# Four graph layers on one core: the statistics' small steps move to GpSimd, the last bias becomes a product with ones, new parts and a new order at both ends

## The chip, the cores and the metric

One of the eight cores of a Trainium2 chip runs the whole program. Its engines are PE (TensorE, products), DVE (VectorE), ACT (ScalarE), POOL (GpSimd) and SP, which here only issues DMAs. The metric is the device time of one execution, in microseconds (us). The kernel before took 1287.67 us (median of three runs, 1285.83 to 1288.37).

## The reference, cut to what matters

128 graphs of 128 nodes with 64 features pass four layers. Each layer normalizes its input, applies ReLU and adds its result to x:

```python
h = maximum(layernorm(x), 0)
x = x + L0(h, adj, ...)      # masked sum over neighbours of relu(x_j A + (x_j - x_k) B + b1), then W2
h = maximum(layernorm(x), 0)
x = x + L1(h, adj, ...)      # three relu(adj @ (h W + b)), then Wout
h = maximum(layernorm(x), 0)
x = x + L2(h, adj, ...)      # y = (adj @ h + h) W + b; y /= |y|; batch norm over ALL graphs; relu
h = maximum(layernorm(x), 0)
x = x + L3(h, adj, ...)      # tanh([h, adj @ h] W1 + b1) W2 + b2
```

Only layer 2 ties the graphs together: its mean and variance (per feature) are over all nodes of all graphs, so nothing after it can start until the last graph's y is there.

## The kernel before, in words

The graphs are taken in 32 groups of four (`G = 4`, `NG = 32`). Three stretches follow each other in time.

**The steady run.** For each group, layer 0 sorts neighbours into one-hot matrices (`sort`, `pick`), projects features (`project`), and then works through 40 half tiles: ACT copies a start value into a bank of PSUM (`fill`), PE adds one-hot products to it (`subtract`), DVE takes the ReLU and adds it to `acc` (`gather`). While a group's half tiles run, layers 1 and 2 of the group before it run in the gaps (`after_layer0`: `layer0_end`, `layer1`, `layer2_norm`). `layer2_norm` ends with `add_sums(ysum, ...)`, which collects the sum of y.

**The drain.** When the last gather has ended, the last group's layers 1 and 2 still have to run. This group (31) is split in two halves of two graphs (`SPLIT = 1`, `first_half`, `second_half`). The variance needs the sum of squares of y minus a shift; the shift is the mean over all but the last `BEHIND` groups (`first_mean`, called when group `NG - 1 - BEHIND` has ended, lines 916 and 967). `squares` (line 938) then takes, for each of the 32 groups in turn, one subtraction on DVE, one Square on ACT (tile `sqv`) and two small products on PE (`add_sums(ysq, ...)`, the groups `blk<-nm,sqv`, four columns wide). `filler` (line 956) puts products without a use between them, and `WARM` more (line 1070) follow the last square; they write to free banks. Then come the constants of the batch norm (`factor`, `summand`, lines 1074 to 1084).

**The last phase.** Per group, `add_normed` (line 1115): POOL multiplies and adds the batch norm's constants (`y<-y,affine_g`, two instructions; group 0 does it on DVE), DVE masks the result into PSUM and adds its ReLU to x (`blk<-y,blk`, `x<-blk,x`) and takes `bn_stats`, which give each half row's mean and sum of squares. The groups are put into parts (`PARTS`, line 63). When the last group of a part has its statistics, lines 1146 to 1152 make variance + eps from them in five small DVE steps plus one for the mean (tile `s`), POOL raises it to the power -0.5 (`rstd<-s,halves`), and DVE makes `less`, the negative mean times that. Then `layer3` (line 1161) runs per group: h is made by four ACT instructions (one per graph) or, where `by_vector(g)` holds, by two DVE instructions that read r and the mean from PSUM (`late_ps`); PE multiplies h with the identity and with adjT (`blk<-ident,h`, `blk<-adjT,h`), ACT copies (`hm`), PE applies W1, ACT takes tanh (`tT`), PE applies W2, DVE adds x (`o`), SP writes it out. The last bias is a product of ones with the bias rows (`biased`), except in groups with `by_vector`, where POOL adds it to x (`x<-x,b3o_all`, line 1173).

**What sets the order.** Every instruction that a generator issues stays in program order on its engine (class `InOrder`, line 93, is why nearly all rows stand under L93). The order between generators is planned: each is a `Stream` with a list of due times, and `run_all` (line 1026) lets the stream with the earliest due time take its next step, as far as its gate is open:

```python
            s = min((s for s in streams if s.gate is None or s.gate()), key=lambda s: s.due())
```

So the lists `NORMED_AT`, `LAYER3_AT`, `SQUARES_PLAN`, `FILLER_PLAN`, `SET_UP_PLAN`, `REST_PLAN` and the entries of `MOVED` and `OWN` (shift, scale or a list of its own for one stage of one group) decide which instruction stands before which on each engine, and nothing else.

Of the kernel before, what the change touches and what calls it, by code (L numbers as in the profile page):

```python
# [9 lines left out]
F32 = mybir.dt.float32  # L10
# [3 lines left out]
AF = mybir.ActivationFunctionType  # L14
ALU = mybir.AluOpType
# [3 lines left out]
P = 128  # L19
F = 64  # L20
G = 4
NP = G // 2
# [18 lines left out]
ORDERS = {0: OTHERS[:FULL] + [k for k in ORDER if k not in OTHERS[:FULL]]}  # L41
NORMED_AT = [6, 110, 533, 764, 800, 1146, 1262, 1575, 1754, 2007, 2324, 2362, 2607, 2739, 2914, 3198, 3445, 3602, 3802, 3991, 4178, 4218, 4630, 4782, 4924, 5115, 5299, 5628, 5841, 5841, 6111, 6391]
LAYER3_AT = [-83, 67, 214, 575, 829, 1011, 1234, 1671, 1717, 1817, 2034, 2268, 2463, 2790, 2929, 3113, 3254, 3424, 3558, 3808, 3842, 4197, 4307, 4590, 4983, 4988, 5425, 5463, 5630, 5934, 6438, 6438]
NORMED_PLAN = [-1449, -256, -191, -49, 328, 438, 883]
LAYER3_PLAN = [1024, 1150, 1834, 1931, 2134, 2139, 2139, 2441, 2441, 2672]
MOVED = {('pick', -1): (0, 0.75), ('pick', -2): (-109, 1.102), ('fill', -1): (18, 0.75), ('fill', -2): (0, 1.021), ('subtract', -1): (-1, 0.752), ('subtract', -2): (21, 0.988), ('gather', -1): (0, 0.75), ('gather', -2): (20, 1.0), ('pick', 0): (-1203, 0.997), ('fill', 0): (-119, 0.877), ('subtract', 0): (-65, 0.947), ('gather', 0): (-52, 0.511), ('sort', 0): (-364, 0.972), ('sort', 1): (-635, 0.697), ('project', 0): (691, 0.585), ('project', 1): (155, 0.997), ('after_layer0', 0): (0, 1.0), ('first_half', -1): (-602, 0.992), ('second_half', -1): (-112, 1.0)}
OWN = {('after_layer0', -2): [-734, -65, 691, 691, 691, 691, 691, 972, 1066, 1154, 1255, 1280, 1280, 1440, 1566, 1644, 1757, 1757, 1940, 1940, 2090, 2450, 2450, 2450, 2450, 2685, 2837, 2881, 3086, 3128, 3145, 3290, 3290, 3290, 3438, 3438, 3592, 3592, 3627, 3646, 3684, 3976, 4078, 4109, 4421, 4485, 4512, 4899], ('first_half', -1): [-1189, -966, -886, -871, -753, -659, -570, -311, -230, -110, -107, -26, -26, 24, 49, 159, 231, 233, 351, 355, 454, 465, 465, 520, 582, 606, 717, 717, 879, 909, 909, 998, 1084, 1149, 1238, 1238, 1283, 1313, 1390, 1404, 1404, 1660, 1664, 1695, 1824, 1984, 2001, 3035], ('second_half', -1): [-1130, -987, -834, -703, -655, -586, -484, -231, -231, -231, -109, -52, -17, 45, 104, 176, 245, 361, 361, 365, 470, 482, 482, 541, 607, 632, 750, 783, 934, 968, 968, 1168, 1168, 1222, 1321, 1321, 1368, 1391, 1493, 1493, 1493, 1734, 1786, 1832, 1980, 2117, 2144, 2459], ('sort', 0): [-361, 30, 30, 595, 607, 607, 738, 738, 860, 860, 860, 1135, 1135, 1235, 1331, 1331, 2024, 2074, 2074, 2134, 2159, 2159], ('project', 0): [-1241, -907, -868, -728, -442, 1053, 1192, 3091, 3728, 3875, 4077, 4162, 4162, 4162, 4182, 4512, 4589, 4619, 4619, 4651, 4662, 4902, 4978, 4996, 5074, 5127, 5127, 5664, 5780], ('pick', -1): [-1123, -774, -706, -706, -634, -425, -425, -96, -84, 631, 881, 881, 896, 1076, 1084, 1544, 1671, 1732, 2021, 2039, 2044, 2391, 2680, 2783, 2937, 3043]}
SET_UP_PLAN = [93, 1417, 1908, 1908, 2104, 2104, 3420, 4777]
PERIOD = 3386
# [6 lines left out]
AFTER_PLAN = [-115, -109, 110, 147, 311, 768, 891, 1024, 1031, 1342, 1462, 1486, 1666, 1825, 1907, 2009, 2138, 2138, 2250, 2401, 2571, 2571, 2663, 2805, 2902, 2973, 3117, 3221, 3537, 3748, 3892, 3907, 4155, 4155, 4155, 4239, 4331, 4381, 4557, 4586, 4665, 4760, 4834, 4915, 5251, 5412, 5494, 5494]  # L56
WARM = 15
BEHIND = 2
SPLIT = 1
REST_PLAN = [-107, -107, 444, 444, 444, 444, 447, 597, 1070, 1895, 2111, 2252, 2268, 2268, 2337, 2501, 2510, 2510, 2510, 2520, 2520, 2945, 2945, 2945, 2991, 3251, 3251, 3251, 3254, 3454, 3584, 3584, 3584, 3584, 3959, 4006]  # L60
SQUARES_PLAN = [2562, 2562, 2682, 2742, 2802, 2858, 2912, 2978, 2978, 3094, 3150, 3273, 3295, 3295, 3411, 3411, 3507, 3882, 3896, 3975, 4046, 4342, 4343, 4343, 4348, 4423, 4452, 4528, 4602, 4678, 4753, 4845, 4891, 4891, 4891, 4891, 4891, 5296, 6393, 6393, 6393, 6393, 6393, 6465, 6756, 6814, 6825, 6942, 7471, 7471, 7572, 7644, 7731, 7826, 7918, 8015, 8114, 8210, 8306, 8306, 8477, 8477, 8635, 9169, 9259, 9350, 9520, 9604, 9604, 9687, 9791, 9826, 9899, 9983, 9996, 10065, 10136, 10136, 10142, 10142, 10142, 10168, 10246, 10246, 11277, 11277, 11277, 11277, 11277, 11277, 11277, 11277, 11277, 11277, 11378, 11378, 11410, 11498, 11538, 11694]
FILLER_PLAN = [3597, 3621, 3621, 3627, 3627, 3786, 3786, 3786, 4060, 4060, 4150, 4150, 4150, 4176, 4545, 4605, 4665, 4665, 4665, 4665]
PARTS = [1, 3, 4, 4, 4, 4, 4, 4, 4]
NBLK = 5
# [44 lines left out]
def network(ctx, tc, io, out, over=None, x1=None):  # L109
# [273 lines left out]
    def bias_all(name, src):  # L383

        n = src.shape[0]
        t = keep.tile([P, n], F32, name=name)
        load_later(t, src.rearrange("(o n) -> o n", o=1).broadcast_to([P, n]))
        return t

    gamma_all = bias_all("gamma_all", io["L2_gnn_gamma"])  # L390
    beta_all = bias_all("beta_all", io["L2_gnn_beta"])
    b3o_all = bias_all("b3o_all", io["L3_gnn_b2"])

# [16 lines left out]
    def over_g(ap):  # L410

        return ap.unsqueeze(1).to_broadcast([P, G, F])
# [5 lines left out]
    def flat(t):  # L418
        return t.rearrange("p a n -> p (a n)")
# [59 lines left out]
    def biased(name, width, pt=None, times=G):  # L479

        pt = bank("ps_pr") if pt is None else pt
        matmul(pt[:, 0 : times * width].rearrange("p (b d) -> p b d", d=width), ones_b, bias(name, times), start=True, stop=False, skip_group_check=True)
        return pt
# [602 lines left out]

    nm_ps, y_ps, late_ps = blks[0][:, 0:P], blks[0][:, P : P + G * F], blks[1][:, 0 : 2 * len(PARTS) * G]
    y_ps = y_ps.rearrange("p (b f) -> p b f", f=F)
# [9 lines left out]
    def by_vector(g):  # L1098
        gs = parts[part_of[g]]
        return len(gs) > 1 and g == gs[-1]  # L1100

# [13 lines left out]
    def add_normed(g):  # L1115
# [28 lines left out]
        s1 = work.tile([P, NG // 4, G], F32, tag="var", name="s1")[:, 0 : len(gs), :]  # L1144
        nc.vector.tensor_tensor(s0, stats[:, :, :, 1], stats[:, :, :, 4], ALU.subtract)
        nc.vector.scalar_tensor_tensor(s0, s0, 0.25, s0, ALU.mult, ALU.mult)
        nc.vector.tensor_tensor(s1, stats[:, :, :, 2], stats[:, :, :, 5], ALU.add)
        nc.vector.scalar_tensor_tensor(s0, s1, 1.0 / F, s0, ALU.mult, ALU.add)
        nc.vector.tensor_scalar(s0, s0, LN_EPS, None, ALU.add)
        nc.vector.tensor_tensor(s1, stats[:, :, :, 1], stats[:, :, :, 4], ALU.add)  # L1150
        if by_vector(g):
            nc.vector.tensor_tensor(late_ps[:, 1, k, :], stats[:, len(gs) - 1, :, 1], stats[:, len(gs) - 1, :, 4], ALU.add)
        yield
        nc.gpsimd.tensor_tensor(r, s0, halves[:, 0 : len(gs), :], ALU.pow)
        yield
        nc.vector.scalar_tensor_tensor(less, s1, -0.5, r, ALU.mult, ALU.mult)
        if by_vector(g):
            nc.vector.tensor_copy(late_ps[:, 0, k, :], r[:, len(gs) - 1, :])
        rooted.add(k)

    def layer3(g):
# [6 lines left out]
        if by_vector(g):  # L1168
            r, less = (late_ps[:, n, part_of[g], :] for n in range(2))
            nc.vector.scalar_tensor_tensor(ys[g], over_f(less), -0.5, xs[g], ALU.mult, ALU.add)  # L1170
            relu_scaled(ys[g], r, h=h)
            yield
            nc.gpsimd.tensor_tensor(xs[g], xs[g], over_g(b3o_all), ALU.add)
        else:
            for b in range(G):
                nc.scalar.activation(h[:, b, :], xs[g][:, b, :], AF.Relu, bias=less3[:, g, b : b + 1], scale=rstd3[:, g, b : b + 1])
                if b == 1:
                    yield
# [19 lines left out]
        tT = work.tile([P, NP, P], F32, tag="tT", name="tT")  # L1198
        nc.scalar.activation(flat(tT), pt[:, 0 : NP * P], AF.Tanh, bias=b3p)
        free_ends.append(pt)  # L1200
        yield ENDS
        po = free_ends.pop(0)
        if not by_vector(g):
            biased("L3_gnn_b2", F, pt=po)
        project_pairs(po, tT, w3o, F, start=by_vector(g))
        headed.add(g)
# [169 lines left out]
```

## Time and profile before

| what | us |
|---|---|
| median of three runs | 1287.67 |
| the profiled execution | 1288.35 |
| its span, first to last instruction | 1286.6 |
| last gather add of group 0, of group 30, of group 31 | 70.51, 1094.27, 1128.87 |
| period of a group in the steady run | 34.07 |
| last product of the squares' sum | 1180.18 |
| first and last POOL instruction of the last phase's powers | 1188.03, 1262.6 |
| last PE product of the last group | 1277.9 |

Busy times over the span: PE 1159.5, DVE 1158.9, ACT 1034.2, POOL 318.4 us. In the last phase, from 1182 to 1287, they are PE 76.7, DVE 78.2, ACT 63.5, POOL 72.7 us. "PEclk" in the profile is the TensorE clock that was granted, 1.00 or 0.50 in every stretch of this trace. A stretch is read by asking which engine's next instruction everyone else waits for; the busy share says where to look, the waits say whether it is so. The second copy of the network in the program (`x1` given) belongs to a branch that these inputs do not take.

### The profile page before, as it was taken

Reading aid. Unit: us, or ns where it says so; the run is one execution under the profiler, and the core shown is the slowest. Engines: PE = TensorE matmul, PEld = TensorE weight load, DVE = VectorE, ACT = ScalarE, POOL = GpSimd, SP = SyncE. Lnnn points to the kernel's source line nnn. Section 1 sums busy time; section 2 is a strip of 40 time slices with the busy share of each in tenths; the row PEclk is TensorE's granted clock in tenths of the full one; section 3 lists DMA queues with packets and bytes.
Section 4 is the critical chain, followed back from the end, with each engine's and each line's share of the span. In section 5 each row is a group of like instructions: output and inputs, shape, how many; then the busy total and the mean of one; then the engine's idle time right before and its main releaser. Section 6 shows DMA issues by size and latency. Waiting matters only on the chain.

```text
span 1286.6 us, 31407 instructions
## 1 busy us (share of the span) xinstructions
PE 1159.5 (90%) x10989; PEld 982.1 (76%) x10990; DVE 1158.9 (90%) x3204; ACT 1034.2 (80%) x2583; POOL 318.4 (25%) x400
## 2 busy tenths in 40 slices
PE   5689999999999999999999999999999999888697
PEld 2568888888877887787878878888878887767576
DVE  6889999999999999999999999999999998845993
ACT  3678888888988888888888888888988888743576
POOL 4241122212121222222211222221211222021992
PEclk9899999999999999999999999999999999995899
DMA  2222222222222222222222222222222212100264
GB/s 80 81 76 70 73 67 73 76 76 77 76 76 69 71 74 66 66 74 71 72 74 71 68 71 72 77 76 76 77 76 67 70 59 61 30 17 1 79 160 128
DMA packets 107012, 92.53 MB, mean 72 GB/s; under 512 B 45135, under 2 KB 90460, under 8 KB 106844
## 3 DMA queue, kind: packets, MB, share of 16 engines
q1 hardware_dynamic: 106380, 90.17, 24.7%
q8 instruction: 89, 1.46, 0.5%
q14 instruction: 79, 0.65, 0.2%
q10 hardware_dynamic: 464, 0.26, 0.1%
HBM read 34.12 MB, written 16.71 MB: 40 GB/s over the span
## 4 chain that ended last, share of the span: by engine, by line
ACT 40%; PE 35%; DVE 16%; issue 4%; POOL 2%; SPq 2%; DMA 1%; DVEq 0%; ACTq 0%; POOLq 0%
ACT blk L93 22%; PE blk L93 14%; PE ps_pr L93 7%; DVE acc L93 4%; ACT extra L93 3%; PE ps_q L93 3%; PE ps_ag L93 3%; ACT dT L93 3%; ACT msg L93 2%; PE ps_ah L93 2%; DVE var L93 2%; ACT psort L93 2%; PE ps_ga L93 2%; PE ps_endps L93 2%; SPq L93 2%
## 5 line engine op out<-in xcount | busy, mean ns | idle before, releaser
L93 DVE SCALAR_TENSOR_TENSOR acc<-blk,acc 128x384 f32<-128x384 f32 x1152 | 590.3, 548 | 28.3 <-PE blk L93 21.0
L93 ACT COPY blk<-psort 128x384 f32<-128x384 f32 x1088 | 497.6, 487 | 14.9 <-DVE acc L93 11.5
L93 PE MATMUL blk<-q,oh 128*128 128x192 bf16 x3072 | 321.9, 248 | 9.2 <-ACT blk L93 4.6
L93 PEld LDWEIGHTS <-oh 128*128 128x128 bf16 x3072 | 262.4, 99 | 43.7 <-issue 30.3
L93 PE MATMUL blk<-near_q,ohn 128*128 128x192 bf16 x1536 | 227.7, 247 | 35.9 <-ACT blk L93 32.3
L93 PEld LDWEIGHTS <-ohn 128*128 128x128 bf16 x1536 | 142.8, 99 | 94.9 <-issue 83.3
L93 POOL TENSOR_TENSOR x<-x,t 128x260 f32<-128x260 f32 (+1 forms) x33 | 23.9, 726 | 426.8 <-DVE t L93 372.7
L93 ACT COPY blk<-psort_r 128x384 f32<-128x384 f32 x192 | 89.1, 490 | 1.9 <-DVE acc L93 0.8
L93 ACT COPY zT<-ps_ga 128x256 f32<-128x256 f32 (+1 forms) x31 | 11.4, 369 | 87.5 <-PE ps_ga L93 87.5
L93 POOL TENSOR_TENSOR y<-y,nrm 128x256 f32<-128x256 f32 x31 | 20.4, 657 | 245.4 <-PE blk L93 214.9
L93 PE MATMUL ps_ag<-adjT,msg 128*128 128x128 f32 x500 | 73.7, 280 | 0.5 <-ACT msg L93 0.5
L93 PE MATMUL ps_pr<-g,dT 128*128 128x128 f32 x496 | 72.9, 279 | 0.3 <-ACT dT L93 0.2
L93 DVE TENSOR_SCALAR ohn<-near_n 128x1536 bf16<-128x1536 bf16 (+1 forms) x132 | 72.0, 546 | 0.0
L93 PEld LDWEIGHTS ps_pr<-g,dT 128*128 128x128 f32 x496 | 65.0, 191 | 4.4 <-ACT dT L93 1.6
L93 PEld LDWEIGHTS ps_ag<-adjT,msg 128*128 128x128 f32 x500 | 63.3, 192 | 0.9 <-ACT msg L93 0.7
L93 ACT ACTIVATE dT<-ps_ag 128x512 f32<-128x512 f32 (+1 forms) x96 | 56.5, 588 | 8.6 <-PE ps_ag L93 8.6
L93 DVE SCALAR_TENSOR_TENSOR h<-x,rstd 128x256 f32<-128x256 f32 (+1 forms) x98 | 51.9, 530 | 9.8 <-PE ps_ga L93 2.0
L93 ACT ACTIVATE sq<-x 128x256 f32<-128x256 f32 (+1 forms) x98 | 40.4, 412 | 25.1 <-DVE x L93 25.0
L93 POOL TENSOR_TENSOR q<-rest,q 128x768 bf16<-128x768 f32 x32 | 52.7, 1648 | 18.2 <-ACT q L93 18.2
L93 PE MATMUL ps_q<-wq,hT 128*128 128x384 f32 x128 | 55.5, 518 | 1.4 <-ACT hT L93 1.4
L93 PE MATMUL ps_p<-wp,hs 128*128 128x384 f32 x128 | 53.8, 503 | 0.1
L93 PE MATMUL ps_sA<-fro,acc 128*128 128x128 f32 x256 | 50.7, 280 | 1.3 <-DVE acc L93 1.3
(267 smaller groups left out, 2605.0 us busy)
## 6 DMA issues: line engine op xcount, KB each, us to landing
near_q<-q SPq DMA_DIRECT2D x288, 63.0 KB
near_n<-n_dram SPq DMA_DIRECT2D x96, 126.0 KB
a<-in_adj_dram SPq DMA_DIRECT2D x32, 256.0 KB
adjT_dram<-adjT SPq DMA_DIRECT2D x32, 256.0 KB
adjT<-adjT_dram SPq DMA_DIRECT2D x32, 256.0 KB
psort_r<-psort SPq DMA_DIRECT2D x32, 228.0 KB
fro_r<-fro SPq DMA_DIRECT2D x32, 152.0 KB
x<-in_x_dram SPq DMA_DIRECT2D x32, 128.0 KB
```

Of the source, the lines that this page charges most:

```text
L93: ins = op(*args, **kw)
```

## The change

Five things are edited.

1. `add_normed`: DVE keeps two of the small steps (the sum of the two halves' squares, now in a tile `s2`, and the sum of the two means); the difference of the means, its square, a scale with eps and the sum with `s2` go to POOL, ahead of the power. All is scaled by F, and tanh's `scale=math.sqrt(F)` undoes it.
2. `by_vector` holds for the odd groups among the last eight (four groups) and no longer for the last group of each of eight parts.
3. The last bias is a product with ones in all 32 groups; the load of `b3o_all` and POOL's eight additions go.
4. `PARTS` has again nine parts, now of 1, 3, 4, 5, 5, 5, 5, 2 and 2 groups.
5. The order: `BEHIND` 2 to 1, `WARM` 15 to 24, all entries of `MOVED` and `OWN` for the last two groups are gone, and new lists stand in `NORMED_AT`, `LAYER3_AT`, `NORMED_PLAN`, `LAYER3_PLAN`, `SET_UP_PLAN`, `REST_PLAN`, `SQUARES_PLAN`, `FILLER_PLAN` and in the entries for groups 0 and 1. The plans of the steady run are not touched.

```diff
...
-WARM = 15
-BEHIND = 2
+WARM = 24
+BEHIND = 1
 SPLIT = 1
...
-PARTS = [1, 3, 4, 4, 4, 4, 4, 4, 4]
+PARTS = [1, 3, 4, 5, 5, 5, 5, 2, 2]
+ENDING = 8
...
-    b3o_all = bias_all("b3o_all", io["L3_gnn_b2"])
...
     def by_vector(g):
-        gs = parts[part_of[g]]
-        return len(gs) > 1 and g == gs[-1]
+        return g >= NG - ENDING and g % 2 == 1
+
+    late_at = {g: n for n, g in enumerate(g for g in range(NG) if by_vector(g))}
...
-        nc.vector.tensor_tensor(s0, stats[:, :, :, 1], stats[:, :, :, 4], ALU.subtract)
-        nc.vector.scalar_tensor_tensor(s0, s0, 0.25, s0, ALU.mult, ALU.mult)
-        nc.vector.tensor_tensor(s1, stats[:, :, :, 2], stats[:, :, :, 5], ALU.add)
-        nc.vector.scalar_tensor_tensor(s0, s1, 1.0 / F, s0, ALU.mult, ALU.add)
-        nc.vector.tensor_scalar(s0, s0, LN_EPS, None, ALU.add)
+        s2 = work.tile([P, NG // 4, G], F32, tag="nrm", name="s2")[:, 0 : len(gs), :]
+        nc.vector.tensor_tensor(s2, stats[:, :, :, 2], stats[:, :, :, 5], ALU.add)
         nc.vector.tensor_tensor(s1, stats[:, :, :, 1], stats[:, :, :, 4], ALU.add)
-        if by_vector(g):
-            nc.vector.tensor_tensor(late_ps[:, 1, k, :], stats[:, len(gs) - 1, :, 1], stats[:, len(gs) - 1, :, 4], ALU.add)
-        yield
+        for q, other in enumerate(gs):
+            if by_vector(other):
+                nc.vector.tensor_tensor(late_ps[:, 1, late_at[other], :], stats[:, q, :, 1], stats[:, q, :, 4], ALU.add)
+        yield
+        nc.gpsimd.tensor_tensor(s0, stats[:, :, :, 1], stats[:, :, :, 4], ALU.subtract)
+        nc.gpsimd.tensor_tensor(s0, s0, s0, ALU.mult)
+        nc.gpsimd.tensor_scalar(s0, s0, 0.25 * F, F * LN_EPS, ALU.mult, ALU.add)
+        nc.gpsimd.tensor_tensor(s0, s0, s2, ALU.add)
         nc.gpsimd.tensor_tensor(r, s0, halves[:, 0 : len(gs), :], ALU.pow)
         yield
         nc.vector.scalar_tensor_tensor(less, s1, -0.5, r, ALU.mult, ALU.mult)
-        if by_vector(g):
-            nc.vector.tensor_copy(late_ps[:, 0, k, :], r[:, len(gs) - 1, :])
+        for q, other in enumerate(gs):
+            if by_vector(other):
+                nc.vector.tensor_copy(late_ps[:, 0, late_at[other], :], r[:, q, :])
         rooted.add(k)
...
-            nc.gpsimd.tensor_tensor(xs[g], xs[g], over_g(b3o_all), ALU.add)
...
-        nc.scalar.activation(flat(tT), pt[:, 0 : NP * P], AF.Tanh, bias=b3p)
+        nc.scalar.activation(flat(tT), pt[:, 0 : NP * P], AF.Tanh, bias=b3p, scale=math.sqrt(F))
...
-        if not by_vector(g):
-            biased("L3_gnn_b2", F, pt=po)
-        project_pairs(po, tT, w3o, F, start=by_vector(g))
+        biased("L3_gnn_b2", F, pt=po)
+        project_pairs(po, tT, w3o, F, start=False)
...
```

In the built order of the changed kernel, engine by engine, the steady run (groups 3 to 29) has the same instructions in the same order. Around the first groups, two more half tiles' products stand on PE ahead of group 1's `ps_num`, and three of the constants' loads stand on SP behind group 1's `n_dram`, `near_n` and `fro_r`. In the drain, both halves of group 31 close layer 0 together after the last gather; the squares come as a block of twelve groups (behind the second product of group 31's layer 1 on PE), then four, two and one, and the last thirteen at the end.

## The prediction, on record before the run

> **What bounds the kernel now.** I read the slices first. PE and DVE stay near full up to slice 37, so the steady run fills nine tenths of the span; the order listing shows it unchanged, and I cost it at nothing: the same instructions in the same order, at 34.07 us a group. What can move is the first 70 us, the drain and the last phase.
>
> ```profile
> PE   5689999999999999999999999999999999888697
> POOL 4241122212121222222211222221211222021992
> PEclk9899999999999999999999999999999999995899
> ```
>
> PEclk falls to 5 where the drain ends, and POOL turns from 2 to 9 right after it. So I asked for busy times by stretch: the last group's gather, the drain to the last y product, the squares, the constants, the last phase to its eighth power, the rest. Columns: length, then PE, PE's weight loads, DVE, ACT, POOL, then the granted clock.
>
> ```profile
> 1094.27:1128.87 34.60, 28.82 (x263) 24.83 (x260) 28.63 (x77) 23.08 (x57) 3.19 (x4) 0.95 0.09 26
> 1128.87:1159.84 30.97, 27.90 (x204) 22.41 (x204) 12.14 (x46) 15.52 (x51) 6.71 (x11) 0.96 0.06 19
> 1159.84:1179.50 19.66, 19.21 (x91) 19.12 (x91) 7.61 (x26) 8.48 (x21) 0.00 (x0) 0.50 0.00 0
> ...
> 1191.12:1256.30 65.18, 50.73 (x629) 43.16 (x630) 59.44 (x254) 45.03 (x115) 60.27 (x66) 0.89 0.45 123
> 1256.30:1286.60 30.30, 22.26 (x294) 19.21 (x293) 10.31 (x41) 17.96 (x46) 4.93 (x4) 0.90 0.47 125
> ```
>
> The third row is PE alone, on the squares at half clock. In the fifth POOL and DVE are both over 90% full and PE is not; in the sixth POOL has almost stopped and PE runs out its backlog. The waits from 1182 on (waiter, what it waited for, total, times, longest) give DVE's part in it:
>
> ```profile
> POOL rstd L93 <- DVE s L93: 6.9, 9, 2.7
> ...
> PE blk L93 <- DVE h L93: 3.1, 2, 1.7
> ...
> PE ps_endps L93 <- DVE h L93: 1.9, 1, 1.9
> ```
>
> **Start: -1 us.** DVE's idle time after 28 us, ahead of its adds, is 3.8 to 4.1 us, most of it one wait for products:
>
> ```profile
> 44.31 0.56 DVE L93 SCALAR_TENSOR_TENSOR acc<-blk,acc 128x384 f32<-128x384 f32 x1 [2.26 <-PE blk L93]
> ```
>
> Two more half tiles now stand on PE ahead of group 1's `ps_num`; two adds (2 x 0.56) fit into the 2.26. Group 1's own chain is the later for it, but it is due a period later. On SP three loads of constants move behind group 1's `n_dram`, `near_n` and `fro_r`, which can only start the sooner. Bounds: all of the idle time gained, -3.8; two half tiles lost again at group 1, +1.
>
> **Drain: +5 us.** The terms, in order.
>
> (a) Last gather. With `BEHIND` 1 the shift is computed after it. Before, it stood inside: PE waited 1.8 us for the sums, DVE 0.7 and 0.6 for the results, and DVE spent 1.4 on its steps, 4.5 us in all. This gather took 34.60, a steady one 34.07, so not all of it cost time; the extra products of the redrawn lists move too. I take -3.5 (bounds -6 and 0).
>
> (b) The squares. Before, a group's four products cost 0.51 in the gaps and 0.853 in the final run:
>
> ```profile
> 1136.81 0.51 PE L93 MATMUL blk<-nm,sqv 128*128 128x4 f32 x4
> ```
> ```profile
> 1161.87 17.17 PE L93 MATMUL blk<-nm,sqv 128*128 128x4 f32 x80
> ```
>
> 80 products in 17.17 us is 0.215 each against 0.13 at full clock. 20 groups were left for the end, now 13. Seven stand earlier, in a block of twelve behind group 31's second layer-1 product. I followed the new order from the gather's end G with durations of before: the last message is ready at G+17.5, the shift at G+19.3, and the block ends at G+26.5 at full clock or G+30.4 at half. The granted clock of before lies at half after clock windows of 3.41 us with 3328 streamed columns or fewer (f32 counted four times), at full after 3620 or more; the block streams 4 columns at a time, so I take most of it at half, G+29. `ps_ag` of layer 1, which is what everything else of group 31 waits for, stands behind it: 29 - 17.5 = 11.5 us late. This is the new wait; queued behind it are ACT's `dT`, the two `gout`, `ga`, `py` and `counted`, and nothing else that could fill PE.
>
> (c) From `ps_ag` to `counted`: 14.4 before (1145.49 to 1159.84) with one half left; now both halves go together, at half clock at first: 17.4 (bounds +1 and +5).
>
> (d) Tail: 13 x 0.853 = 11.1 and 2.0 for the last products, where 20 x 0.853 and 2.3 stood.
>
> The sum: G + 17.5 + 11.5 + 17.4 + 13.1 = G+59.5, against 51.3 before, which is +8.2; less 3.5 of (a) +4.7, taken as +5. The bounds: block at full clock (-4), chain +1 instead of +3 (-2), and the gather's -6 with one more for the tail's first products at full clock, -6.6 in all; the other way +1.4, +2 and +3.5, +11.6. The 24 fills of `WARM` cost nothing as long as they end ahead of the first h, which came 10.4 us behind the last `own` product (1180.2 to 1190.6); 24 at some 0.3 are 7 to 8.5.
>
> The Trainium skill says, in "TensorE: Matmul & The Clock Gate", Part 1, that the half clock comes after an idle window of about 3.4 us. The trace differs: the clock stood at half from 1157.4 to 1184.7 while PE was recorded 98% busy, on products four columns wide. By the page's words the block would run at full clock and the sum would be 3 to 4 us less.
>
> **Last phase: -1 us.** POOL's side first:
>
> ```profile
> L93 POOL TENSOR_TENSOR y<-y,affine_g 128x256 f32<-128x256 f32 x62 | 44.2, 730 | 27.3 <-DVE affine_g L93 25.5
> L93 POOL TENSOR_TENSOR rstd<-s,halves 128x16 f32<-128x16 f32 x7 | 20.4, 2910 | 5.8 <-DVE s L93 5.8
> ```
>
> y stays. Powers of 4, 12 and 16 elements took 1.04, 2.28 and 2.91, so 0.156 an element: 20 make 3.54, 8 make 1.66 (estimates), and the nine parts sum to 23.7 as before. The eight bias additions go, -5.5. New are 9 x 4 = 36 small steps. POOL's small steps of before are at the start:
>
> ```profile
> 4.32 0.19 POOL L93 TENSOR_TENSOR caps<-caps,in_n 128x2 f32<-128x2 f32 x1
> 4.61 0.21 POOL L93 TENSOR_SCALAR in_n<-neg_p 128x1 f32<-128x1 f32 x1
> ```
>
> From start to start 0.29, so 10.4 us; with 20 elements instead of 2 and DVE beside them they may take 0.7 (DVE's own step with 16 elements took up to 0.74 while POOL ran y), 25 us. I take 0.29, from the nearer row. POOL: 44.2 + 23.7 + 10.4 = 78.3, plus 3.3 to 5 of waits where 6.9 stood, from 1182.5 on: the last power ends at 1264.6 to 1266 (1262.6 before).
>
> The Trainium skill's "GPSIMD Engine Reference", section 4.1, speaks against this move: two-input steps belong on VectorE, since GpSimd is about half as fast. DVE's steps here came 0.20 apart when undisturbed; twice that is 14.4 us, 4 more than above.
>
> DVE: per part it loses four steps of some 0.3, it makes h for four groups instead of eight (0.84 each), and has no other new work than two small copies per such group: 78.2 becomes about 62.7. It is no longer near the bound; `blk`, `x` and `stats` follow y without queue. PE's 5.0 us of waits for DVE's h go for about half, since POOL's pace (78.3/32 = 2.45 a group) is now what is late next and PE needs 2.2 to 2.3.
>
> ACT gets four more groups' h at 1.46, 5.8 us, in part hidden: it had 63.5 of 105 us. The eight bias products more on PE (0.11 to 0.28 each) cost 1 to 2 us of its sum. PE's backlog at the end: before, the eighth power ended at 1256.3 with eight groups' work left, 1256.3 + 8 x 2.2 = 1273.9 against 1277.9 measured; now the sixth is estimated at 1244.5 with fourteen left, 1275.3. That is +1.4; with -2.5 of the waits, -1. Bounds -5 (all waits gone, POOL no later) and +6 (small steps at 0.45 with no wait saved).
>
> **Sum.** -1 + 5 - 1 = +3 on the profiled 1288.35 (span 1286.6 and 1.75 around it): 1291.4. The median is 0.7 less than that execution; I leave it in.
>
> **Rivals.**
> 1. *DVE was the bound, and the change frees it* (faster, about 1282). For it: `DVE s` is 5.4% of the last 187 us' chain, 10 us, and each part's six steps take up to 2.3 us there, stretched beside POOL's y. If the chain per part gets 0.6 to 1 us shorter, nine parts and the 2.5 of the h give -8; drain +3, start -1: 1282.4. It decides if the last power ends by 1262. Against it: POOL is 92% full already, and it gets more.
> 2. *No measurable difference* (within 0.2%, 2.6 us, about what a measurement of this kernel tells from no change): the block runs at full clock and term (b) shrinks by 4, the rest as forecast: 1287.5. That the change does not do what it says would look the same: the steps leave DVE, whose wait was covered anyway.
> 3. *POOL's small steps are slow* (slower, about 1299): at 0.5 each beside a busy DVE, 36 cost 18 us instead of 10.4; POOL is full from 1191 on, so the last power ends at 1273 and, with the drain's +5, the end comes 10 us later. It decides from 0.4 a step on. For it: DVE's small steps stretched from 0.17 to 0.74 beside y; against it: POOL's y itself shows 0.71 to 0.77 with DVE busy or idle.
>
> **Chances.** The forecast (+2.6 to +8) 0.34, rival 3 and a drain at its upper bound 0.13, rival 2 0.22, rival 1 0.31. So slower 0.47, same 0.22, faster 0.31. The range reaches to rival 1's middle and to rival 3: 1280 to 1299.
>
> **What would show it.** Start: the 2.26 ahead of the add at 44.31 gone and group 0's last add before 70.5. (a): the last gather 34 us or less from the one before. (b): one block of 48 `sqv` products before group 31's `ps_ag`, at 0.21 each if the half clock holds, 0.13 if not; the last `own` product at G+59.5. Last phase: the small steps at 0.29, the powers of 20 at 3.5, the last power at 1266 plus the drain's shift, and PE's waits for DVE's h at half. I am wrong if the block ends before the last message needs PE, or if PE is not the last engine to run out after the last power.

## The result, and the profile after

The changed kernel took 1300.75 us (median of five runs, 1299.76 to 1301.55) against 1288.37 for the kernel before in the same job: ratio 1.0099, 95% interval 1.0085 to 1.0114. It is slower by about 12.5 us, where +3 was forecast and 1299 was the end of the range. The profiled execution has a span of 1299.8 us, 13.2 more than before.

The same slices of the page, of the kernel after:

```profile
PE   5689999999999999999999999999999999796786
...
POOL 3331112222121211222222221112222122014981
PEclk7799999999999999999999999999999999976898
```

In slice 39, the middle of the last phase, PE and POOL both read 8 where they read 9, and in slice 40 PE has 6 for 7: both have become less busy in a phase that has become longer. The stretches that answer to those of before (last gather; drain to the last y product; the last squares; the last phase from the first h product to the eighth power; the rest), same columns:

```profile
1093.72:1129.11 35.39, 28.60 (x264) 24.75 (x262) 27.78 (x69) 24.16 (x57) 3.19 (x4) 0.95 0.09 26
1129.11:1170.31 41.20, 37.59 (x235) 31.32 (x233) 16.14 (x59) 18.52 (x58) 6.63 (x11) 0.79 0.06 14
1170.31:1183.48 13.17, 12.62 (x58) 12.53 (x58) 5.21 (x19) 5.43 (x14) 0.00 (x0) 0.50 0.00 0
1193.78:1268.51 74.73, 56.70 (x683) 47.70 (x683) 52.27 (x214) 54.76 (x146) 65.51 (x91) 0.86 0.41 112
1268.51:1299.80 31.29, 20.16 (x248) 17.07 (x246) 10.97 (x36) 13.21 (x31) 3.88 (x8) 0.84 0.41 109
```

Read the lengths first. Drain and squares together are 54.4 us (50.6 before), the phase up to the eighth power 74.7 (65.2 before). In that row POOL was busy 60.3 of 65.2 us before and is busy 65.5 of 74.7 now: its work grew by 5.2 us, and its idle time nearly doubled, from 4.9 to 9.2 us. DVE fell from 59.4 to 52.3 us of work, in a longer stretch. POOL's share fell from 92% to 88%, so no engine has become the bound by being full. The waits of the kernel after, from 1182 on, say what fills the gaps:

```profile
ACT h L94 <- DVE less L94: 26.5, 5, 8.2
...
DVE less L94 <- POOL rstd L94: 18.0, 9, 3.2
...
POOL s L94 <- DVE stats L94: 7.4, 6, 2.4
...
PE ps_endps L94 <- ACT hm L94: 4.0, 1, 4.0
...
PE blk L94 <- DVE h L94: 2.6, 1, 2.6
```

The second line did not exist before: at each of the nine powers DVE stands and waits for POOL. The third is POOL waiting for DVE. The two wait for each other in turn, and behind them wait ACT's h (18.4 us for `less` before, 26.5 now) and PE.

A fixed point makes runs comparable: the end of the last `ident,own` product (the squares' sum is there), and from it to the end of the last `o` on DVE. The 13.2 us split into the last gather's end +0.24 (1128.87 to 1129.11), from there to that product +3.8 (51.3 to 55.1), from it to the last `o` +8.7 (98.8 to 107.5), and +0.5 behind that. Each value of this measure comes from one profiled execution. Three kernels with the last phase of before gave 98.8, 98.3 and 97.9, and four with that of after 107.2 to 108.0, so a difference of less than 1 us says nothing. The device times of the kernel before scatter more, from 1285.7 to 1290.5 us over its executions.

### The profile page after: what moved, and what is told of

Same layout as the page of the kernel before. It is cut to its first block, busy times and chain, and to the rows that moved or that the text cites. A ratio compares the mean times of both kernels' runs of the same rounds, so it can differ in the third digit from the quotient of the medians.

```text
span 1299.8 us, 31438 instructions
## 1 busy us (share of the span) xinstructions
PE 1167.3 (90%) x11006; PEld 988.0 (76%) x11007; DVE 1147.5 (88%) x3152; ACT 1038.2 (80%) x2599; POOL 322.3 (25%) x428
## 4 chain that ended last, share of the span: by engine, by line
ACT 38%; PE 32%; DVE 18%; issue 6%; POOL 3%; SPq 2%; DMA 1%; DVEq 0%; ACTq 0%; POOLq 0%
ACT blk L94 20%; PE blk L94 13%; PE ps_pr L94 6%; DVE acc L94 4%; PE ps_q L94 3%; ACT extra L94 3%; PE ps_ag L94 3%; ACT msg L94 2%; PE ps_ah L94 2%; ACT dT L94 2%; DVE var L94 2%; ACT psort L94 2%; PE ps_ga L94 2%; POOL rstd L94 2%; SPq L94 2%
## 5 line engine op out<-in xcount | busy, mean ns | idle before, releaser
L94 PE MATMUL blk<-q,oh 128*128 128x192 bf16 x3072 | 322.2, 249 | 11.2 <-ACT blk L94 4.3
L94 ACT ACTIVATE sq<-x 128x256 f32<-128x256 f32 (+1 forms) x98 | 40.1, 410 | 30.8 <-DVE x L94 27.7
L94 ACT ACTIVATE h<-x,less,rstd 128x64 f32<-128x64 f32 x112 | 40.9, 435 | 28.8 <-DVE less L94 26.5
```

Source lines behind the costliest of these rows:

```text
L94: ins = op(*args, **kw)
```

## The experiments

| kernel | ratio to before, 95% interval | own to last o, us | DVE's wait for rstd, us |
|---|---|---|---|
| before | | 98.8 | 0 |
| after | 1.0099 (1.0085 to 1.0114) | 107.5 | 18.0 |
| new start | 0.9989 (0.9975 to 1.0003) | 98.3 | 0 |
| new drain | 1.0024 (1.0015 to 1.0034) | 97.9 | 0 |
| new last phase | 1.0151 (1.0128 to 1.0175) | 107.2 | 18.0 |
| before, steps on POOL | 1.0047 (1.0028 to 1.0066) | 102.5 | 4.0 |
| before, bias product | 0.9988 (0.9975 to 1.0000) | 96.9 | 0 |
| after, steps on DVE | 1.0078 (1.0057 to 1.0100) | 104.4 | 10.3 |
| after, parts of before | 1.0107 (1.0090 to 1.0125) | 105.8 | 18.1 |
| after, lists of normalisation and parts of before | 1.0058 (1.0043 to 1.0073) | 101.5 | 10.6 |
| after, all four lists and parts of before | 1.0031 (1.0018 to 1.0044) | 100.2 | 7.9 |
| before, one list of after | 1.0077 (1.0060 to 1.0094) | 108.6 | 8.4 |

**1 to 3: which end of the kernel.** Start alone:

```diff
-SET_UP_PLAN = [93, 1417, 1908, ...]
+SET_UP_PLAN = [-291, 1261, 1323, ...]
-REST_PLAN = [-107, -107, 444, ...]
+REST_PLAN = [4, 6, 632, ...]
...
```

and so on for the entries of groups 0 and 1 in `MOVED` and `OWN`.

> The kernel before with the new lists of the start alone (set-up, rest, groups 0 and 1). The profile after ends group 0's gather 0.55 us later and group 1's 0.23 sooner than before. Theory (start costs nothing): within 1 us of before. Rival (a start that is later shifts all that follows): +1 to +3 us.

Group 0 ended at 70.25, group 1 at 102.93 (105.26 before), ratio 0.9989. DVE's wait of 2.26 us at 44.31 became one of 1.01. The gain is 1.4 us by the ratio, with an interval that still holds zero; the rival is out. Drain alone:

```diff
-WARM = 15
-BEHIND = 2
+WARM = 24
+BEHIND = 1
...
```

with `SQUARES_PLAN` and `FILLER_PLAN` of after, and without the entries of the last two groups in `MOVED` and `OWN`.

> The kernel before with the drain redrawn alone (shift over all but the last group, 24 fills, the new lists of squares and fills, no own entries for the last two groups). In the profile after the last own product ends 4.05 us later than before, at 1184.23. Theory (the drain is a loss of its own that adds to the last phase's): last own product 4 us later than before, time +3 to +5 us. Rival (the last phase has slack for it): own product 4 us later, time within 1.5 us of before.

The gather ended at 1126.95, 1.9 us sooner than before, but 1.35 of that were there when group 30 ended (1092.92 for 1094.27), in a stretch whose order is that of before. The last own product came at 1182.06, 1.9 later, as 55.1 us lay between. Time +3 us. The drain is a loss of its own. The last phase alone:

```diff
-PARTS = [1, 3, 4, 4, 4, 4, 4, 4, 4]
+PARTS = [1, 3, 4, 5, 5, 5, 5, 2, 2]
+ENDING = 8
-    b3o_all = bias_all("b3o_all", io["L3_gnn_b2"])
...
```

with the four lists of that phase, the steps, the bias and `by_vector` of after.

> The kernel before with the last phase changed alone: small steps on GpSimd, bias as a product, new parts, DVE's h for other groups, new lists of that phase. In the profile after the stretch from the last own product to the last o is 8.7 us longer. Theory (the last phase carries two thirds of the loss, whatever the drain does): +7.5 to +10 us. Rival (the new last phase was drawn for the new drain and loses only behind it): +2 to +5 us.

From own to the last o it took 107.2 us: the loss is there without the new drain. But the ratio of 1.0151 holds another 8 us from the start, which I had not foreseen: with the load of the bias rows gone, the set-up has a step less, the later ones each take an earlier place in the old plan, and DVE waited 9.48 us for one row of constants (0.57 before):

```profile
51.29 0.21 DVE L94 TENSOR_REDUCE cat<-cat 3x1 f32<-3x64 f32 x1 [9.48 <-DMA cat<-in_L_gnn_bout_dram]
```

Group 0 ended at 78.94. From here on the load stays, unused, wherever the old start is combined with the new bias.

**4: is it lost in `after` too?** The kernel after with the load kept:

```diff
+    b3o_all = bias_all("b3o_all", io["L3_gnn_b2"])
```

> The kernel after with the load of the bias rows kept, unused, as last of the later loads, as in the kernel before. Group 0 and 1 ended at 71.06 and 105.03 after, but at 70.25 and 102.93 with the new lists of the start and the load kept. Theory (the load's removal moves every later step of the set-up to another place in the plan, and that is where the gain of the start went): group 1 ends at about 103, time 1 to 2.5 us less than after. Rival (the start's difference is chance of one execution): within 0.7 us of after.

Group 1 ended at 103.93, ratio 1.0098 (1.0075 to 1.0121): the time did not move, so the theory fell. With the new lists of the start, group 1 ended between 102.75 and 105.03 in fourteen profiled executions, with the load and without, 102.75 to 102.93 in ten of them; the 105.03 of after was the latest.

**5 and 6: the small steps.** On the kernel before:

```diff
-        nc.vector.tensor_tensor(s0, stats[:, :, :, 1], stats[:, :, :, 4], ALU.subtract)
-        nc.vector.scalar_tensor_tensor(s0, s0, 0.25, s0, ALU.mult, ALU.mult)
...
+        nc.gpsimd.tensor_tensor(s0, stats[:, :, :, 1], stats[:, :, :, 4], ALU.subtract)
+        nc.gpsimd.tensor_tensor(s0, s0, s0, ALU.mult)
...
```

> The kernel before with the four small steps per part on GpSimd alone; its parts, its h on DVE, its bias additions and its order are those of before. 36 steps at 0.29 us start to start make POOL's own work 10.4 us longer. Theory (the loss of the last phase comes from the parts and the order, 5 5 5 5 2 2, whose round trips between POOL and DVE no longer overlap): +0 to +3 us, the steps' time taken from POOL's 6.9 us of waits and DVE's freed time. Rival (POOL is full, so its added work is the loss): +6 to +9 us, last power 6 to 9 us later.

Own to the last o went from 98.8 to 102.5, the last power from 82.4 (84.0 in the runs of the start and of the drain alone) to 88.2 us behind own, the time up by 6 us: nearer to the rival, POOL had little room. Its waits did shrink: 6.9 us for DVE's `s` before, 2.2 for `stats` here. The price of a step was that of the prediction, 0.29 to 0.32 from start to start and 2.91 for the power, here in this kernel:

```profile
1225.98 0.24 POOL L93 TENSOR_TENSOR s<-stats 128x16 f32<-128x16 f32 x1
1226.30 0.22 POOL L93 TENSOR_TENSOR s<-s 128x16 f32<-128x16 f32 x1
1226.60 0.20 POOL L93 TENSOR_SCALAR s<-s 128x16 f32<-128x16 f32 x1
1226.89 0.22 POOL L93 TENSOR_TENSOR s<-s,s 128x16 f32<-128x16 f32 x1
1227.19 2.91 POOL L93 TENSOR_TENSOR rstd<-s,halves 128x16 f32<-128x16 f32 x1
```

The other way round, in the kernel after:

```diff
-        nc.gpsimd.tensor_tensor(s0, stats[:, :, :, 1], stats[:, :, :, 4], ALU.subtract)
...
+        nc.vector.tensor_tensor(s0, stats[:, :, :, 1], stats[:, :, :, 4], ALU.subtract)
...
```

> The kernel after with the four small steps per part back on DVE, scaled as before; everything else as after. From the last own product to the last o: 98.8 us before, 102.5 with the steps on GpSimd alone, 107.5 after. Theory S (the steps' place and the new parts are two losses that add): 103 to 104.5, time 3 to 4.5 us less than after. Rival P (the parts of five and two set the pace by their round trips, wherever the steps run): 106 to 109, time within 1.5 us of after. Rival D (DVE needs the relief): more than 109.

104.4: theory S. The steps cost 3.1 us here and 3.7 to 4.6 there (102.5 against the three values from 97.9 to 98.8). The time, though, fell only by a ratio of 1.0099 to 1.0078, about 2.7 us, with overlapping intervals; the row of the last phase is the better witness.

**7 and 8: the bias as a product, and a version that beats both.**

```diff
-            nc.gpsimd.tensor_tensor(xs[g], xs[g], over_g(b3o_all), ALU.add)
-        if not by_vector(g):
-            biased("L3_gnn_b2", F, pt=po)
+        biased("L3_gnn_b2", F, pt=po)
```

> The kernel before with the last bias as a product in all 32 groups and GpSimd's eight additions gone; the load of the bias rows stays, unused, so that the set-up keeps its order. Theory A (POOL's pace sets the last phase, 5.5 us of its work go, 3.9 of it ahead of the last power): last power 2 to 4 us sooner, time -1.5 to -4 us. Theory B (PE's backlog sets the end, so POOL's relief is worth nothing and eight more products cost): 0 to +1.5 us.

Own to the last o 96.9, 1.0 to 1.9 less; the eighth power came 1.3 us sooner and the ninth 0.4. Ratio 0.9988 (0.9975 to 1.0000): the time is at the low end of theory A, but its last power, 2 to 4 us sooner, did not come. POOL's additions went, and its waits for DVE's `s` rose from 6.9 to 9.8 us. With the new start as well:

> As the kernel with the bias as a product and the unused load kept, with the new lists of the start added, which alone gave a ratio of 0.9989. If the two are independent: the sum of both, -3 to -6 us by theory A of the bias, -0.5 to -2 us by theory B.

Ratio 0.9979 (0.9967 to 0.9990), 2.7 us less than before, between the two forecasts; it is the lowest ratio of this study and faster than both kernels. Own to the last o 96.9 again, group 1 at 102.76.

**9: the choice of groups whose h DVE makes**, on that kernel:

```diff
-        gs = parts[part_of[g]]
-        return len(gs) > 1 and g == gs[-1]
+        return g >= NG - ENDING and g % 2 == 1
```

> The kernel with the new lists of the start and the bias as a product (load kept), and now h on DVE for every other of the last eight groups, four instead of eight. 96.9 us from own to the last o without this edit. Theory (DVE is the bound up to the eighth power and loses 4 x 0.84 of work, ACT has room): 95.5 to 97. Rival (ACT's four more groups at 1.46 us each stand in PE's way): 97.5 to 100.

97.5 us, ratio 0.9988 (0.9978 to 0.9998): at the border of the two expectations, and no gain that could be measured.

**10 to 12: the parts.** My first theory of the remaining loss was the two short parts at the end, each with a round trip of its own (POOL, kernel after):

```profile
1259.70 3.55 POOL L94 TENSOR_TENSOR rstd<-s,halves 128x20 f32<-128x20 f32 x1
1263.22 1.53 POOL L94 TENSOR_TENSOR y<-y,affine_g 128x256 f32<-128x256 f32 x2
1265.72 0.21 POOL L94 TENSOR_TENSOR s<-stats 128x8 f32<-128x8 f32 x1 [0.97 <-DVE stats L94]
...
1268.48 1.53 POOL L94 TENSOR_TENSOR y<-y,affine_g 128x256 f32<-128x256 f32 x2
1272.41 0.21 POOL L94 TENSOR_TENSOR s<-stats 128x8 f32<-128x8 f32 x1 [2.40 <-DVE stats L94]
```

One group's y, a wait for DVE, a power, the next group's y, a wait. Merged:

```diff
-PARTS = [1, 3, 4, 5, 5, 5, 5, 2, 2]
+PARTS = [1, 3, 4, 5, 5, 5, 5, 4]
```

> The kernel after with its last two parts of two groups made one part of four (1 3 4 5 5 5 5 4); lists, GpSimd's steps and all else as after. From the power of group 28 to that of group 32 it took 6.3 us before and 12.0 after. Theory R (a part's y may only be issued once the part before the last has its rstd, so the two short parts at the end run one round trip of POOL, DVE, POOL after the other): one round trip less, last power 2 to 4 us sooner, from own to the last o 104 to 106 instead of 107.5, time -1.5 to -3.5 us against after. Rival B (PE's backlog of nine groups sets the end, the last power is early enough): time within 1 us of after.

The last power came 90.2 us behind own instead of 91.0, own to the last o stayed at 107.8, ratio 1.0093 (1.0071 to 1.0116): theory R fell. With the last y brought forward too:

```diff
-NORMED_AT = [..., 6242, 6248, 6518, 6847]
+NORMED_AT = [..., 6000, 6100, 6200, 6300]
```

> As the kernel with the last part of four, and the normalisation of the last four groups given earlier due times, so that POOL makes five and a half groups' y ahead of the sixth five-group power and only half a group's after it. Theory R: a further 1 to 3 us less to the last power, 102 to 105 from own to the last o. Rival Y (the y that are brought forward delay the power of groups 23 to 27, for which PE waits): no gain over the merged part, or up to 2 us more.

108.5 us, ratio 1.0126 (1.0107 to 1.0146): the power of groups 23 to 27 came 1.9 us later, as rival Y had it. The parts of before in the kernel after:

```diff
-PARTS = [1, 3, 4, 5, 5, 5, 5, 2, 2]
+PARTS = [1, 3, 4, 4, 4, 4, 4, 4, 4]
```

> The kernel after with the parts of before (1 3 4 4 4 4 4 4 4); its lists, its steps on GpSimd, its h on DVE for every other of the last eight groups as after. The steps on GpSimd alone gave 102.5 from own to the last o, the bias as a product took 1.9 off (98.8 to 96.9). Theory K (the sizes of the parts are the remaining 7 us): 100 to 103, time 4 to 7 us less than after. Rival O (the new order of the lists is it, since POOL has y only two groups ahead at each power where before had three to four): 105 to 108, time within 2 us of after.

105.8: rival O. Part sizes by themselves are at most 1.7 us, and the times do not show them: the ratio is 1.0107 (1.0090 to 1.0125), no lower than that of after, and the profiled execution, at 1296.71 us, was the fastest of four (the others 1300.33 to 1302.31).

**13 to 17: the order.** In the built order of before, POOL has 4, 8, 12, 16, 20, 24, 28, 32 and 32 groups' y made when it comes to the nine powers: always a whole part ahead, so that DVE has that part's `blk`, `x` and `stats` to do while POOL raises to the power. After, the lead is 3, 7, 10, 15.5, 20, 26, 30, 31, 32 for parts that end with 1, 4, 8, 13, 18, 23, 28, 30 and 32 groups. One number first:

```diff
-NORMED_PLAN = [-1606, -170, -126, -89, 175, 181, 411]
+NORMED_PLAN = [-1606, -170, -126, -89, 175, 181, 800]
```

> The kernel after with one number changed: the due time of the step that issues a part's small GpSimd steps and power, 411 to 800 (before: 883). In the built order POOL then has 4, 8, 12, 18, 21, 28, 30, 32, 32 groups' y made ahead of the nine powers, where after had 3, 7, 10, 15.5, 20, 26, 30, 31, 32 and before 4, 8, 12, ... 32, 32. Theory L (the lost lead of the y is the open 5 us: POOL and DVE wait for each other in turn): DVE's waits for rstd, 18.0 us after, fall below 8, and own to the last o falls from 107.5 to 102.5 to 105.5. Rival H (the choice of groups for DVE's h, or the sizes of the parts): above 106.5.

108.5 us, ratio 1.0104 (1.0087 to 1.0121): theory L failed here. DVE's wait for rstd fell from 18.0 to 9.6 us, but POOL's y now waited 6.9 us for DVE to be done with an older y, and the power of the first five-group part ended 44.5 us behind own instead of 40.0. The same with the parts of before:

> As the kernel with 411 changed to 800, and with the parts of before. Theory L: 101 to 104 from own to the last o, part sizes worth 1 to 2 us as without it. Rival H: 104.5 to 106, as with the parts of before alone (105.8).

104.1, ratio 1.0074 (1.0054 to 1.0094), at the upper end of theory L: 1.7 us better than the parts alone, 4.4 better than the number alone. The two go together. The lead alone is not all: this kernel has that of before but for one group at the eighth power (31 for 32), and DVE still waits 11.9 us for rstd. Then all four lists and the parts of before, with the steps on GpSimd, the bias product and the new choice of h left in:

```diff
-PARTS = [1, 3, 4, 5, 5, 5, 5, 2, 2]
+PARTS = [1, 3, 4, 4, 4, 4, 4, 4, 4]
-NORMED_PLAN = [-1606, -170, -126, -89, 175, 181, 411]
+NORMED_PLAN = [-1449, -256, -191, -49, 328, 438, 883]
...
```

> The kernel after with the parts and the four lists of the last phase of before; the steps on GpSimd, the bias as a product and DVE's h for every other of the last eight groups stay. Theory L: what is left are the steps' +3.7 and the bias' -1.9, so 100 to 102 from own to the last o. Rival H (the choice of groups is the open 5 us): 104 to 107.

100.2 us: theory L. What is left over before is the steps' +3.7 and the bias' -1.9, 100.6 by sum. Of these lists, those of the normalisation alone:

> The kernel after with the parts and the two lists of the normalisation of before; the two lists of layer 3 stay as after. POOL's lead at the powers is 4, 8, 12 ... 32, 32 again. Theory N (the order of the normalisation's steps, POOL's and DVE's, is all that the order costs): 100 to 101.5 from own to the last o. Rival 3 (the lists of layer 3, which put h, hm, tT and o between them, carry the 4 us): 103 to 105.

101.5 us: theory N, at the edge. The lists of layer 3 carry 1.3, the order of the normalisation with its parts 6.0; by the ratios, 1.0031, 1.0058 and 1.0099, it is 3.5 and 5.3. Against after, POOL's gaps up to the last power fell from 13.1 to 7.9 us, and that power came 5.5 us sooner behind own: up to there the order's price is these waits. What lies between 104.1 and 101.5 is in the other entries of the two lists, which set when y, the mask, the statistics and the small steps stand; it was not divided further. POOL's row of this kernel shows the lead at work, eight instructions of y behind the seventh power, then the small steps of the eighth with no wait:

```profile
1249.76 2.91 POOL L94 TENSOR_TENSOR rstd<-s,halves 128x16 f32<-128x16 f32 x1
1252.64 5.77 POOL L94 TENSOR_TENSOR y<-y,affine_g 128x256 f32<-128x256 f32 x8
1258.37 0.24 POOL L94 TENSOR_TENSOR s<-stats 128x16 f32<-128x16 f32 x1
...
1259.58 2.91 POOL L94 TENSOR_TENSOR rstd<-s,halves 128x16 f32<-128x16 f32 x1
1265.49 0.25 POOL L94 TENSOR_TENSOR s<-stats 128x16 f32<-128x16 f32 x1 [3.00 <-DVE stats L94]
```

And from the other side, the kernel before with one list of after and nothing else:

```diff
-NORMED_PLAN = [-1449, -256, -191, -49, 328, 438, 883]
+NORMED_PLAN = [-1606, -170, -126, -89, 175, 181, 411]
```

> The kernel before with one list of seven numbers from after, that of the steps of a group's normalisation; steps on DVE, parts, bias and all other lists as before. POOL then has 3, 7, 10, 14.5, 18, 22, 27, 31, 32 groups' y ahead of the powers. Theory L: own to the last o rises from 98.8 to 102 to 105, DVE waits for rstd where it did not wait at all. Rival H: 98 to 100.5.

108.6 us, 10 more, beyond theory L's own range and far from the rival's. The waits of this kernel:

```profile
POOL x L93 <- DVE y L93: 15.8, 6, 8.8
...
POOL rstd L93 <- DVE s L93: 10.3, 8, 3.0
...
DVE less L93 <- POOL rstd L93: 8.4, 6, 2.9
...
PE blk L93 <- DVE h L93: 7.3, 3, 4.9
```

No step was moved between engines and no part changed. The list sets a group's y a little later, and its statistics, small steps, power and `less` sooner, the power most (883 to 411). The mutual wait is there, and the kernel takes 10 us longer by it. But that is not the price in after: the last power came 9.2 us later, and POOL's gaps ahead of it grew by 9.1, of which 5.3 stand at bias additions that wait for DVE's first step of an h (part of the first line shown), a step that after does not have.

**18: the drain.**

```diff
-BEHIND = 1
+BEHIND = 2
```

> The kernel after with the shift taken over all but the last two groups again, inside the last gather; the lists stay. In the built order the block of twelve groups of squares then falls apart into pieces of two to six products between the last group's other work, and thirteen groups stay for the end. After: gather ends at 1129.11, last own product 55.1 us later (before: 51.3). Theory (the block at half clock and the late shift are the drain's loss): own 50 to 53 us behind the gather's end, gather at most 1 us later, time -2 to -4 us against after. Rival (the last thirteen groups at half clock and the two halves going together are it): 54 to 56 us, time within 1 us of after.

Neither: the last gather took 42.7 us instead of 35.4, and own stood 54.8 behind its end. The block of squares did fall apart, but the shift's products and the waits about them (DVE 1.9 us for the node counts, PE 1.4 for DVE's `own`, among others) now stood inside a gather whose order had no place kept for them, with the granted clock at 0.84 over that stretch. Ratio 1.0159 (1.0139 to 1.0179). So the late shift is not the drain's whole loss, and BEHIND 2 is only as good as the entries that before had for it. Which part of the 3.8 us lies in the block and which in the two halves that close together was not separated, so the drain's cause stays open.

## Why the prediction was wrong, point by point

**Start, -1: right in kind.** -1.4 us alone, not quite clear of zero; the wait at 44.31 shrank as forecast, from 2.26 to 1.01.

**Drain, +5 with the start's -1 beside it: right in sum, by two errors that cancel.** Own came 4.05 us later than before; the forecast had +4. But term (a), the last gather, was to gain 3.5 and gained nothing: 35.39 us in after and 34.03 with the drain alone, where before took 34.60; kernels with the new drain and BEHIND 1 took 34.0 to 36.2, those with the old one 33.2 to 35.4. The wait of PE for the shift's sums went, and another took its place: `ps_ah` of group 30's layer 1 stood in PE's queue ahead of its h (2.6 us). With it came a clock window of 2304 streamed columns (f32 counted twice), the half clock from 1109.0 to 1112.4 (before, it stood from 1123.3 to 1126.7), and 2.49 us in which DVE had no products. Term (b) was too dear: the block ended at G+26.2, not G+29. Its row:

```profile
1146.55 8.78 PE L94 MATMUL blk<-nm,sqv 128*128 128x4 f32 x48 [1.28 <-ACT sqv L94]
```

48 products at 0.183: the granted clock was full until 1149.9, half from there. Term (c) measured 15.1 instead of 17.4, and (d), to the last own product, 13.9 instead of 13.1. G+55.1 instead of G+59.5. The lower bound of -6.6 is not the sum of its terms, 8.2 - 4 - 2 - 6 - 1 = -4.8.

The rule for the clock behind (b) needs two corrections. In the kernel before, windows with up to 3328 streamed columns came ahead of half clock and those with 3584 or more ahead of full, but with f32 counted twice, not four times. In the kernel after even that does not part them: 4608 columns in the window from 1269.4 were followed by half, 2816 in that from 1143.1 by full. So it describes one trace and is no rule to plan by.

**Last phase, -1 with bounds -5 and +6: this step failed.** It measured +8.7. Of its terms:

- The POOL prices held: 0.29 to 0.32 from step to step (0.29 forecast), 3.54 and 1.65 for the new powers (3.54 and 1.66 forecast). Rival 3 named the right time, 1299, for the wrong reason: no step took 0.5.
- POOL's waits did not. "Plus 3.3 to 5 of waits where 6.9 stood" was a guess that fewer DVE steps mean fewer waits. POOL waited 7.4 us for `stats` alone, and its gaps up to the last power sum to 13.1 us (8.7 before), some 3 of them the spaces around the small steps. With the normalisation's order and parts of before, and the steps on POOL as well, it waited 3.0 us for `stats`. The last power came 91.0 us behind own, where the forecast's 1264.6 to 1266, on before's own at 1180.2, was 84.4 to 85.8 (1182.5 + 78.3 + 3.3 to 5 gives 0.2 to 0.5 less).
- "It is no longer near the bound; `blk`, `x` and `stats` follow y without queue" is the sentence that was wrong. DVE had less to do (52.3 us for 59.4 up to the eighth power), but its queue is in order, and `less` stands in it directly behind the small steps: DVE waited 18.0 us for powers with the next part's work behind it, and POOL then waited for that work. The built order of the changed kernel has the lead of 3, 7, 10 in place of 4, 8, 12; the forecast only added up POOL's instructions.
- "1244.5 with fourteen left, 1275.3" took PE's backlog for granted. PE had none: it had used up the 18 groups it had been given when the sixth power, that of groups 18 to 22, ended (66.7 us behind own; 64.3 was forecast). It stood idle 4.0 us there, 3.7 at the fourth power and 2.6 at 1269, and the fourteen groups took some 40 us instead of 30.8. In sum PE idled 21.3 us between its first h product and the last o (15.1 before), and was busy 76.6 (72.7). Its waits for DVE's h fell to about half, from 5.0 to 2.6, as forecast, but those for ACT's h and hm rose from 11.2 to 18.8. Each of the three idle stretches was followed by a window of 3.41 us at half clock, from 1225.0, 1252.4 and 1272.8 (0.86 and 0.84 on average in the last two stretches, 0.89 and 0.90 before).
- The bias product was a gain of 1.0 to 1.9 us, where I had put the eight products at a cost of 1 to 2 and the eight additions only into POOL's sum.

**The account.** From own to the last o: 98.8, +3.7 for the steps, -1.9 for the bias, gives 100.6 (100.2 measured); +1.3 for layer 3's lists, little more than the measure's scatter; +6.0 for the order of the normalisation with its parts: 107.5. The last 6.0 do not split into a price for the parts and one for the plan: the parts alone, put back, gave 1.7, which the times do not show, and one number of the plan alone -1.0.

**The rules weighed.** The row first: on 128x16 elements POOL's step took 0.20 to 0.24 and came 0.29 to 0.32 behind the last, DVE's 0.16 to 0.17 and 0.20. The Trainium skill's "GPSIMD Engine Reference", section 4.1, puts a factor of about 2 between them; here it is 1.5, and the advice held: the move cost 3.1 to 4.6 us. DVE's waiting also had a second price. `less` took 0.17 to 0.19 in six of the nine rows of before and 0.35 to 0.40 in the other three. After, it took 0.68 to 0.70 in eight of nine: there it starts as the power ends, which is when POOL's next y (0.72 to 0.73) starts. The ninth, with nothing behind it on POOL, took 0.17:

```profile
1263.28 0.70 DVE L94 SCALAR_TENSOR_TENSOR less<-s,rstd 128x20 f32<-128x20 f32 x1 [2.12 <-POOL rstd L94]
1268.54 0.68 DVE L94 SCALAR_TENSOR_TENSOR less<-s,rstd 128x8 f32<-128x8 f32 x1 [0.54 <-POOL rstd L94]
1275.23 0.17 DVE L94 SCALAR_TENSOR_TENSOR less<-s,rstd 128x8 f32<-128x8 f32 x1 [1.84 <-POOL rstd L94]
```

The Trainium skill's "SBUF — State Buffer", section "Who interferes with whom", says that a DVE instruction with two inputs in SBUF contends with a GpSimd instruction that reads there, and calls the shared ports an exclusive lock. These rows agree: the step ends with the y beside it. It is half a microsecond between a power and its h.

## What to carry to other kernels

Where two engines with in-order queues hand work to each other part by part, count from the built order how much of the next part each has done when it comes to the hand-over. Here the busy shares did not show whether they overlap or take turns, and the order did; the lead was part of it: put back alone it gave nothing, and with the parts of before 1.7 us. The work taken from DVE, over 90% full, was worth nothing here: its queue then waited for the engine that got the work. And a backlog that the last stage had before is to be worked out anew from the times at which its input now arrives, before it is used to bound the end.

## What the runs showed that was not expected

A removed load can cost more than it saves: under the old plan it moved each later step of the set-up and left DVE 9.48 us without a row of constants. A part's power costs 1.04, 1.65, 2.28, 2.91 and 3.54 us for 4, 8, 12, 16 and 20 elements per partition, a straight line of 0.156 an element. The granted clock lagged by a window: the block of squares began in one with 192 streamed columns (f32 counted twice) at full clock, and it fell to half only in the next.
